# Layer-0 cross-attention prepared in eight pieces beside the units, the next stage's rows beside the last units, and a turned threshold search in a four-layer decoder

## The chip, the core and the metric

The kernel runs on one core of one Trainium2 chip. The metric is the device time of one execution in microseconds (us), and the median over several runs. The engines are named as in the profile: PE (matrix multiplications, with its weight loads as PEld), DVE (vector), ACT (scalar, activation tables), POOL (general purpose) and SP (which here issues transfers). They run side by side, each through its own queue in order, and wait for one another through semaphores. Matrix products land in PSUM, the other tiles lie in SBUF.

## The reference, cut to what matters

A decoder of four layers; each layer adds a self-attention, a cross-attention to a context and a feed-forward part to x, each behind a normalization. x is 16 sequences of 128 tokens with 256 features, the context 16 x 128 x 192, everything float32. The change touches the cross-attention and feed-forward part of layer 0, and the cross-attention and the feed-forward part of layer 2.

```
# layer 0, cross-attention (16 heads of 16); query is layernorm(x), key = value = context
Qp = query @ Wq + bq
K = _l2norm(key @ Wk + bk);  V = value @ Wv + bv;  Q = _l2norm(Qp)
scores = jnp.einsum('bhqd,bhkd->bhqk', Q, K) * SCALE
attn = jax.nn.softmax(scores, axis=-1)
out = ... einsum('bhqk,bhkd->bhqd', attn, V) ... @ Wo + bo
x = out + Qp
return (x - mu) / jnp.sqrt(var + LN_EPS) * ln_gamma + ln_beta

# layer 2, feed-forward: each of 8 experts takes the 256 tokens that score highest for it
probs = jax.nn.softmax(xt @ Wg, axis=-1)
_, top_idx = jax.lax.top_k(probs.T, cap)            # cap = 2048 // 8
tok2exp = where(assigned, argmax(masked, axis=0), argmax(pT, axis=0))
h = jax.nn.gelu(xt @ W1[e], approximate=False) @ W2[e]   # times the gate of the token
```

The feed-forward part of layer 0 has 32 routed experts of width 128 and one shared one, applied to all tokens and weighted per token.

## The kernel before

The 16 sequences are blocks of 128 tokens (a tile `self.x[g][:, t, :]` of 128 partitions by 256); four blocks are a group, so there are `NG` = 4 groups of `GB` = 4 blocks. Stages run one after the other. The framework schedules the instructions of each engine from the program's order and their dependencies; instructions recorded with `pinned` or `pinned_transpose` keep the program's order on PE, those of `mm` and `transpose_group` may be moved.

**Layer-0 attention.** `staggered` walks over the 16 blocks ("units"). For unit n it issues the scores (`scores16`, tile st16), then parts of older units, then the exponentials on ACT, then the first part of the combination of unit n-1. `combine16` is a generator with four parts: values times weights (o16, copied to oT by ACT), the turn back (o16t, `rsum` and `c` on DVE), the next turn (ctr, copied to cT by DVE), and the output projection (proj). One whole group is prepared by `prologue(g + 1)` at the third unit of group g. In the cross-attention, `prologue` computes the keys kT and the lengths of their rows (squares on ACT, `ksum` by products with a column of ones, `over_length`), the values (`values32`), the normalized rows h and their transposes hT, the queries qp with their squares on ACT, their lengths, the unit rows u on POOL (`nc.gpsimd.tensor_scalar`, line 530), and their transposes qm. After the last block of a group, `done` normalizes the group on DVE and ACT and runs three additions or products over the group on POOL (lines 548 to 550), of which the last updates x.

**Layer-0 feed-forward.** `tokens(g)` normalizes a group and turns it; `first` computes gate and up products of an expert for a group, `router` the weights, `second` the down product. `tokens(0)` and `tokens(1)` stand at the head of the stage, `tokens(2)` and `tokens(3)` behind the first two routers.

**Layer-2 cross-attention** (`xattn64`, 8 heads, 16 units) takes an optional `begin`, which returns work to be issued beside given units; here it is called without it.

**Layer-2 feed-forward** (`l2_ffn`) writes zeros to the DRAM rows `hs` (23 blocks), normalizes the groups into `hall`, turns them, and computes the logits with the tokens on the partitions (16 products of 8 columns a group, of two records each in the trace). After the softmax it seeks for each expert the largest bit pattern `thr` that at least 256 probabilities reach, two bits a step, 15 steps:

```python
nc.vector.tensor_tensor(mask, p3 (x3), cand.bitcast(F) (x16), ALU.is_ge)     # 128 x 384, bf16
self.mm(ps, [(onesb, mask)])                                                 # sum over the partitions
nc.vector.tensor_reduce(count, ps, AX.X, ALU.add)                            # sum over the 16 blocks
```

followed by three small operations on `count`, `step` and `thr` and one on `cand`. Then `ranks` numbers the chosen tokens, POOL scatters the rows of `hall` to `hs` (16 indirect transfers), and `fetch` reads blocks of `hs` in fours and the expert's weights W12 block by block.

Two pools matter: `slot` hands out one of 7 weight slots in rotation (tag w8), and `b1` one of 4 PSUM banks.

Of the kernel before, what the change touches and what calls it, by code (L numbers as in the profile page):

```python
# [16 lines left out]
P = 128  # L17
B = 16
# [11 lines left out]
class Decoder:  # L30
    def __init__(self, ctx, tc, a, out):
# [8 lines left out]
        self.flip = 0  # L40

# [218 lines left out]
    def values32(self, wk, pairs, bias):  # L260

        nc = self.nc
        v = wk.tile([P, 16, 32], F, tag="v32", name="v32", bufs=6)
        nc.gpsimd.memset(v[:, :, 16:32], 0.0)
        nc.gpsimd.memset(v[:, :, 16:17], 1.0)
        ps = self.b1("v")[:, 0:DM]
        self.mm(ps, pairs)
        nc.vector.tensor_tensor(
            v[:, :, 0:16], ps.rearrange("p (h d) -> p h d", h=16), bias.rearrange("p (h d) -> p h d", h=16), ALU.add
        )  # L270
        return v
# [107 lines left out]
    def staggered(self, prologue, maxima, scores, exponentials, combine):  # L379
# [3 lines left out]
        state = {0: prologue(0)}  # L383
# [7 lines left out]
        for n in range(B + 3):  # L391
            g, t = divmod(n, GB)
            if n < B:
                st = scores(state[g], t)
            part(n - 3)
            part(n - 2)
            if n < B:
# [6 lines left out]
            last = es  # L404
            part(n - 2)
            if t == GB - 2 and g + 1 < NG:
                state[g + 1] = prologue(g + 1)

# [75 lines left out]
    def l0_xattn(self):  # L484
# [5 lines left out]
        def over_length(n, scale):  # L490

            nc.vector.tensor_scalar(n, n, 1e-24, None, ALU.max)
            nc.scalar.activation(n, n, AF.Sqrt, scale=scale)
            nc.vector.reciprocal(n, n)

        with self.tc.tile_pool(name="l0x", bufs=1) as wk:
            bq, bv, bo = (self.brow(wk, f"L0_xattn_{n}") for n in ("bq", "bv", "bo"))

            def prologue(g):

                kT = wk.tile([P, 2, GT], F, tag="kT", name="kT", bufs=2)
                sq = self.hp.tile([P, 2, GT], F, tag="hT", name="ksq", bufs=5)
                for half in range(2):
                    ps = self.b1("kT")
                    self.mm(ps, self.ctx_l(wk_, half * P, (half + 1) * P, slice(g * GT, (g + 1) * GT)))
                    nc.vector.tensor_scalar(kT[:, half, :], ps, self.c("L0_xattn_bk")[:, half : half + 1], None, ALU.add)
                    nc.scalar.activation(sq[:, half, :], kT[:, half, :], AF.Square)
                ps = self.b1("ksum")[:, 0:GB]
                for t in range(GB):
                    self.mm(ps[:, t : t + 1], [(sq[:, half, T4(t)], self.ones[:, 0:1]) for half in range(2)])  # L510
                rk = self.small([P, GB], "rk")
                nc.vector.tensor_copy(rk, ps)
                over_length(rk, 16.0)
                v = [
                    self.values32(wk, self.ctx_r(wv, 0, DM, slice(g * GT + t * P, g * GT + (t + 1) * P)), bv)
                    for t in range(GB)
                ]
                hT = self.hidden_T(self.layernorm(g))
                qp = wk.tile([P, GB, DM], F, tag="qp", name="qp", bufs=2)
                n = self.small([P, GB], "l2n")  # L520
                junk = wk.tile([P, DM], BF, tag="junk", name="junk", bufs=1)
                for t in range(GB):
                    ps = self.b1("qp")[:, 0:DM]
                    self.mm(ps, [(hT[:, k, T4(t)], wq[:, k, :]) for k in range(2)])
                    nc.vector.tensor_tensor(qp[:, t, :], ps, bq, ALU.add)
                    nc.scalar.activation(junk, qp[:, t, :], AF.Square, accum_out=n[:, t : t + 1])
                over_length(n, 1.0)
                u = self.hp.tile([P, GB, DM], F, tag="h", name="unit", bufs=2)
                for t in range(GB):
                    nc.gpsimd.tensor_scalar(u[:, t, :], qp[:, t, :], n[:, t : t + 1], None, ALU.mult)  # L530
                qm = wk.tile([P, 2, 2, GT], F, tag="qm", name="qm", bufs=2)
                for half in range(2):
                    ps = self.b1("utr")
                    for t in range(GB):
                        nc.tensor.transpose(ps[:, T4(t)], u[:, t, half * P : (half + 1) * P], self.ident)
                    nc.vector.tensor_scalar(qm[:, half, 0, :], ps, self.par[:, 0:1], None, ALU.mult)
                    nc.scalar.activation(qm[:, half, 1, :], ps, AF.Copy, scale=self.par[:, 1:2])
                nc.gpsimd.tensor_tensor(qp, qp, bo.unsqueeze(1).to_broadcast([P, GB, DM]), ALU.add)
                return qm, kT, rk, v, qp

            def combine(s, g, t, es):
# [18 lines left out]
                combine,  # L560
            )

    def l0_ffn(self):
# [20 lines left out]
        with self.tc.tile_pool(name="l0f", bufs=1) as wk:  # L584
# [3 lines left out]
            hTs = []  # L588

            def tokens(g):  # L590
                st = self.small([P, GB, 6], "bnst")
                mv = self.small([P, GB, 2], "bnmv")
                rs = self.small([P, GB], "rstd")
                nm = self.small([P, GB], "nmean")
                for t in range(GB):
                    nc.vector.bn_stats(st[:, t, :], self.x[g][:, t, :])
                    nc.vector.bn_aggr(mv[:, t, :], st[:, t, :])
                self.rsqrt(rs, mv[:, :, 1])
                nc.vector.scalar_tensor_tensor(nm, mv[:, :, 0], -1.0, rs, ALU.mult, ALU.mult)
                h = self.hp.tile([P, GB, DM], F, tag="h", name="h", bufs=2)  # L600
                for t in range(GB):
                    nc.scalar.activation(
                        h[:, t, :], self.x[g][:, t, :], AF.Identity, scale=rs[:, t : t + 1], bias=nm[:, t : t + 1]
                    )
                hT = self.hp.tile([P, 2, GT], F, tag="hT", name="hT", bufs=5)
                for k in range(2):
                    ps = self.b1("tr")
                    for t in range(GB):
                        self.pinned_transpose(ps[:, t * P : (t + 1) * P], h[:, t, k * P : (k + 1) * P])
                    nc.scalar.copy(hT[:, k, :], ps)  # L610
                hTs.append(hT)
# [81 lines left out]
            tokens(0)  # L693
            tokens(1)
            for e in range(-1, E):
                for g in range(NG):
# [4 lines left out]
                    if e < 0:  # L701
                        router(g)
                        if g + 2 < NG:
                            tokens(g + 2)
# [975 lines left out]
    def l2_xattn(self):  # L1680
        self.xattn64(8, [f"L2_xattn_{n}" for n in ("Wq", "Wk", "Wv", "Wout")], "L2_xattn_bout", "l2x")

    def l2_ffn(self):
# [7 lines left out]
        wg = self.wp.tile([P, 2, E], F, tag="wg2", name="wg2")  # L1691
        self.load_into(wg, "L2_ffn_Wg")
        hs = self.tc.dram_tile([NB * P, DM], F, name="hs")
        ys = self.tc.dram_tile([NB * P, DM], F, name="ys")
        with self.tc.tile_pool(name="l2f", bufs=1) as wk:
            tile_ = lambda shape, name, dt=F, bufs=1: wk.tile(shape, dt, tag=name, name=name, bufs=bufs)
            zero = tile_([P, DM], "zero")
            nc.gpsimd.memset(zero, 0.0)
            for b in range(NB):
                nc.sync.dma_start(out=hs[b * P : (b + 1) * P, :], in_=zero)  # L1700
# [5 lines left out]
            bits = tile_([P, 15, 3, E], "bits", I32)  # L1706
            for i in range(15):
                for j in range(3):
                    nc.gpsimd.memset(bits[:, i, j, :], (j + 1) << (2 * i))
# [15 lines left out]
            h = tile_([P, B, DM], "hall")  # L1725
            logits = self.b1("logits")[:, 0 : B * E]
            for g in range(NG):
                hg = h[:, g * GB : (g + 1) * GB, :]
                self.norm_tokens(self.x[g], hg)
                hT = self.hidden_T(hg)  # L1730
                for t in range(GB):
                    o = (g * GB + t) * E
                    self.mm(logits[:, o : o + E], [(hT[:, k, t * P : (t + 1) * P], wg[:, k, :]) for k in range(2)])

            p3 = tile_([P, B, E], "p3")
            flat = lambda a: a.rearrange("p t e -> p (t e)")
            m = self.small([P, B], "m16")
            l3 = logits.rearrange("p (t e) -> p t e", e=E)
            nc.vector.tensor_reduce(m, l3, AX.X, ALU.max)
            bcast = lambda a: a.unsqueeze(2).to_broadcast([P, B, E])  # L1740
            over_t = lambda a: a.unsqueeze(1).to_broadcast([P, B, E])
            nc.vector.tensor_tensor(p3, l3, bcast(m), ALU.subtract)
# [7 lines left out]
            thr = tile_([P, E], "thr", I32)  # L1750
            nc.vector.memset(thr, 0)
            cand = tile_([P, 3, E], "cand", I32)
# [683 lines left out]
```

## Time and profile before

| | |
|---|---|
| median of 3 runs | 3641.01 us (3630.87 to 3645.12) |
| the profiled execution | 3646.33 us, of which the span is 3644.6 us |
| mean granted clock of TensorE | 0.948 |
| busy: PE, DVE, ACT, POOL | 3348.9, 2113.7, 1421.1, 456.9 us |
| instructions in the span | 51429 |
| layer-0 cross-attention, first kT to first gate | 181 to 380 us |
| layer-2 cross-attention to the first block of its feed-forward | 2065 to 2361 us |

The page gives the busy time of each engine, a strip of 40 equal slices, and the groups of instructions with their mean duration and what ended the idle time before them. The chain of waits follows the execution back from its last instruction. A window adds up the busy time of a stretch; its granted clock is 1.00 at full speed.

### The profile page before, as it was taken

The numbers are of one execution on the slowest core, as the hardware profiler recorded it, in microseconds if no ns is written. First come the engines' busy times: TensorE is split into PE (matmuls) and PEld (weight loads), VectorE is DVE, ScalarE is ACT, GpSimd is POOL, SyncE is SP. The second block draws the span as 40 slices with busy tenths as digits, with TensorE's granted clock in tenths as the row PEclk, the third lists the DMA queues.
The fourth block names the chain that finished last, engine by engine and source line by source line (L and its number), as shares of the span: only waits on it lengthen the run. The fifth ranks groups of instructions, "written<-read, shape, count | busy, mean of one in ns | idle before, by whom it ended". The sixth has DMA issues, their size and how long they took to land.

```text
span 3644.6 us, 51429 instructions
## 1 busy us (share of the span) xinstructions
PE 3348.9 (92%) x20976; PEld 1807.7 (50%) x20976; DVE 2113.7 (58%) x4137; ACT 1421.1 (39%) x1910; POOL 456.9 (13%) x627
## 2 busy tenths in 40 slices
PE   7888999999998899998999999196999999999999
PEld 4655555555556656665455566062122222224656
DVE  5535544444463544458777644425899999963440
ACT  3344411111124422228555322023577777783221
POOL 5423100000002221110000110104000000002100
PEclk9988999999998999999999998597799999999989
DMA  3000000000010000010000001374212020000000
GB/s 98 1 10 1 14 18 22 18 22 18 26 54 1 28 11 1 1 30 20 12 1 12 2 1 34 121 238 115 49 26 31 11 31 11 11 1 25 1 8 18
DMA packets 90484, 105.46 MB, mean 29 GB/s; under 512 B 11364, under 2 KB 72678, under 8 KB 89990
## 3 DMA queue, kind: packets, MB, share of 16 engines
q1 hardware_dynamic: 79672, 89.71, 9.3%
q0 software_dynamic: 4224, 6.43, 0.5%
q10 hardware_dynamic: 6352, 6.03, 0.5%
q8 instruction: 165, 2.70, 0.3%
q14 instruction: 71, 0.58, 0.1%
HBM read 85.53 MB, written 16.60 MB: 28 GB/s over the span
## 4 chain that ended last, share of the span: by engine, by line
PE 79%; DVE 10%; ACT 5%; issue 3%; POOL 2%; DMA 1%; SPq 0%; POOLq 0%; ACTq 0%; DVEq 0%
PE acc L1968 7%; PE down L255 6%; PE gate L255 6%; PE up L255 6%; PE proj L255 6%; PE st L1968 5%; PE one L1968 4%; PE qT L166 4%; PE st L255 4%; PE o L255 2%; PE h L255 2%; DVE mx L2114 2%; PE rb L255 2%; PE v L948 2%; PE fc L166 2%
## 5 line engine op out<-in xcount | busy, mean ns | idle before, releaser
L2114 DVE TENSOR_REDUCE mx<-one 128x1 f32<-128x512 f32 x1024 | 659.0, 686 | 62.4 <-PE one L1968 53.1
L2251 ACT ACTIVATE e<-st 128x1024 f32<-128x1024 f32 x512 | 497.0, 1021 | 214.4 <-PE st L1968 213.4
L674 ACT ACTIVATE gs<-gate,cols 128x512 f32<-128x512 f32 x132 | 90.7, 687 | 552.7 <-PE gate L255 552.6
L1968 PE MATMUL acc<-e,v 128*32 128x512 f32 x2048 | 289.6, 615 | 0.9 <-ACT e L2251 0.9
L688 DVE SCALAR_TENSOR_TENSOR x<-down,w_all,x 128x256 f32<-128x256 f32 x512 | 212.4, 478 | 111.1 <-PE down L255 110.9
L1968 PE MATMUL st<-qp,kp 113*128 113x512 bf16 x1024 | 274.5, 389 | 2.3 <-ACT e L2251 1.9
L255 PE MATMUL down<-expert,gs 128*128 128x256 f32 x1056 | 251.0, 381 | 2.2 <-DVE gs L675 2.2
L255 PE MATMUL gate<-hT,expert 128*128 128x512 f32 x528 | 250.3, 596 | 0.0
L255 PE MATMUL up<-hT,expert 128*128 128x512 f32 x528 | 248.7, 593 | 0.0
L255 PEld LDWEIGHTS down<-expert,gs 128*128 128x128 f32 x1056 | 201.4, 191 | 86.1 <-issue 61.5
L675 DVE SCALAR_TENSOR_TENSOR gs<-up,cols,gs 128x512 f32<-128x512 f32 x132 | 99.0, 750 | 230.0 <-PE up L255 229.9
L1968 PE MATMUL one<-kp,qp 16*128 16x512 bf16 x1024 | 211.9, 400 | 4.0 <-DVE mx L2114 2.6
L1968 PEld LDWEIGHTS <-qp 16*128 16x128 bf16 x1024 | 48.9, 91 | 333.4 <-issue 328.5
L255 PEld LDWEIGHTS up<-hT,expert 128*128 128x128 f32 x528 | 100.8, 191 | 127.2 <-issue 126.9
L1968 PEld LDWEIGHTS <-kp 113*128 113x128 bf16 x1024 | 79.2, 98 | 140.9 <-issue 82.6
L1048 ACT COPY rb<-rb 128x512 f32<-128x512 f32 x64 | 37.5, 586 | 258.9 <-PE rb L255 258.9
L1050 DVE TENSOR_TENSOR cT<-o,rb 128x512 f32<-128x512 f32 x64 | 44.3, 691 | 157.1 <-ACT rb L1048 157.1
L255 PEld LDWEIGHTS gate<-hT,expert 128*128 128x128 f32 x528 | 100.4, 192 | 70.5 <-issue 64.0
L166 PE MATMUL qT<-hT,L_xattn_Wq 128*128 128x512 f32 x256 | 114.1, 599 | 6.6 <-DVE hT L110 4.5
L255 PE MATMUL o<-e,v 128*32 128x128 f32 (+1 forms) x2048 | 105.6, 280 | 11.8 <-DVE nm L292 11.8
L1357 DVE SCALAR_TENSOR_TENSOR xs<-xBC,cols,xs 128x508 f32<-128x508 f32 x144 | 106.0, 741 | 12.4 <-ACT xs L1353 9.1
L962 POOL CAST kb<-kT 128x512 bf16<-128x512 f32 x64 | 41.5, 676 | 433.6 <-DVE kT L110 433.6
(522 smaller groups left out, 5512.1 us busy)
## 6 DMA issues: line engine op xcount, KB each, us to landing
W<-in_L_ffn_W_dram SPq DMA_DIRECT2D x46, 512.0 KB, 5.5
expert<-in_L_ffn_Wg_dram SPq DMA_DIRECT2D x32, 128.0 KB, 2.2
expert<-in_L_ffn_Wu_dram SPq DMA_DIRECT2D x32, 128.0 KB, 2.3
expert<-in_L_ffn_Wd_dram SPq DMA_DIRECT2D x32, 128.0 KB, 2.3
parts<-parts SPq DMA_DIRECT2D x16, 256.0 KB, 2.5
qp<-parts SPq DMA_DIRECT2D x28, 128.0 KB, 3.7
kp<-parts SPq DMA_DIRECT2D x12, 256.0 KB, 7.7
hs<-zero SPq DMA_DIRECT2D x23, 128.0 KB, 1.9
```

Source lines behind the costliest of these rows:

```text
L166: self.nc.tensor.matmul(out, lhsT, rhs, start=i == 0, stop=i == n - 1 and bias is None)
L255: self.tc.keep_in_program_order(self.nc.tensor.matmul(*a, **k))
L674: nc.scalar.activation(gs, pg, AF.Silu, bias=bg)
L675: nc.vector.scalar_tensor_tensor(gs, pu, bu, gs, ALU.add, ALU.mult)
L688: nc.vector.scalar_tensor_tensor(xt, pd[:, t, :], w_all[:, o : o + 1], xt, ALU.mult, ALU.add)
L948: nc.tensor.matmul(ps, l, r, start=True, stop=False)
L962: nc.gpsimd.tensor_copy(kb[:, i + j, :], kT[:, i + j, :])
L1050: nc.vector.tensor_tensor(cT, po, rb, ALU.mult)
L1357: stt = lambda *a: pin(nc.vector.scalar_tensor_tensor(*a))
L1968: self.tc.keep_in_program_order(nc.tensor.matmul(*a, **k))
L2114: nc.vector.tensor_reduce(mx[:, t, kc, i : i + 1], pair[i], AX.X, ALU.max)
L2251: nc.scalar.activation(e[:, 2 * p : 2 * p + 2, :], ps, AF.Exp, scale=1.0 / 16.0)
```

## The change

1. `staggered` accepts a `prologue` that is a generator. For each unit of group g two pieces of the prologue of group g + 1 are issued: one between the older units' parts and the exponentials, one behind the combination's first part; what is left is issued at the group's last unit. `beside` holds further work for given units.
2. The prologue of the layer-0 cross-attention is cut into eight pieces by `yield`. All its products are pinned. The statistics of two groups are taken together; the key lengths and query lengths share one square root; the unit rows are on DVE instead of POOL; `qp` lies in two of the weight slots.
3. `tokens` of the layer-0 feed-forward becomes the method `l0_ffn_rows`; groups 0 and 1 are issued beside units 13 and 14 of the cross-attention.
4. `l2_ffn_begin` is passed to the layer-2 cross-attention: it issues the zero writes, takes two weight slots for `hall`, and returns the statistics, rows and logits of groups 0 to 2 for the units 10, 11, 12, 14 and 15. The logits have the experts on the partitions (`lT`, 32 rows a group) and are turned back once. Group 3 is done at the head of `l2_ffn`.
5. The search runs on the turned probabilities `pT` (one partition for each pair of block and expert, 128 tokens along the row); the count over the row comes from the compare's accumulator, the sum over the 16 blocks from one product with `same`.
6. The count of `above` is one product instead of `ranks`; `fetch` reads the first block of `hs` alone and then fours.

```diff
 # staggered
+            ahead = not whole and g + 1 < NG
+            if ahead and t == 0:
+                pieces = prologue(g + 1)
             if n < B:
                 st = scores(state[g], t)
             part(n - 3)
             part(n - 2)
+            if ahead:
+                piece(g + 1)
             if n < B:
                 es = exponentials(state[g], t, st, nm)
...
             last = es
+            if ahead:
+                piece(g + 1)
             part(n - 2)
-            if t == GB - 2 and g + 1 < NG:
+            if whole and t == GB - 2 and g + 1 < NG:
                 state[g + 1] = prologue(g + 1)
+            while ahead and t == GB - 1 and g + 1 not in state:
+                piece(g + 1)
+            for work in (beside or {}).get(n, ()):
+                work()
 # l0_xattn, prologue
+                if g in (0, 2):
+                    stats([g, g + 1])
+                mv, rs = rows[g]
...
-                    self.mm(ps, self.ctx_l(wk_, half * P, (half + 1) * P, slice(g * GT, (g + 1) * GT)))
+                    products(ps, self.ctx_l(wk_, half * P, (half + 1) * P, slice(g * GT, (g + 1) * GT)))
...
                     nc.scalar.activation(sq[:, half, :], kT[:, half, :], AF.Square)
+                    yield
...
+                nc.vector.tensor_scalar(n[:, 0], ps, 1e-24, 16.0, ALU.max, ALU.mult)
+                yield
+                if g % 2 == 0:
+                    qps.append(self.slot([P, 2, GB, DM], "qp"))
...
-                over_length(n, 1.0)
+                nc.vector.tensor_scalar(n[:, 1], n[:, 1], 1e-24, None, ALU.max)
+                nc.scalar.activation(n, n, AF.Sqrt)
+                nc.vector.reciprocal(n, n)
                 u = self.hp.tile([P, GB, DM], F, tag="h", name="unit", bufs=2)
                 for t in range(GB):
-                    nc.gpsimd.tensor_scalar(u[:, t, :], qp[:, t, :], n[:, t : t + 1], None, ALU.mult)
+                    nc.vector.tensor_scalar(u[:, t, :], qp[:, t, :], n[:, 1, t : t + 1], None, ALU.mult)
...
+                yield
...
+                {13: [lambda: self.l0_ffn_rows(0)], 14: [lambda: self.l0_ffn_rows(1)]},
 # l2_ffn_begin
+        h = [self.slot([P, 8, DM], "hall") for _ in range(2)]
...
+            r = slice(32 * g, 32 * g + 32)
+            ps = self.b1("lT")
+            for k in range(2):
+                self.pinned(ps[r, :], wg[:, k, :], hT[:, k, :], start=k == 0, stop=k == 1)
...
+        st["last"] = [lambda: stats([3]), lambda: rows(3), lambda: logits(3)]
+        return {
+            10: [at(stats, [0, 1]), at(rows, 0)],
+            11: [at(rows, 1), at(logits, 0)],
+            12: [at(logits, 1)],
+            14: [at(stats, [2]), at(rows, 2)],
+            15: [at(logits, 2)],
+        }
 # l2_ffn
+            ps = self.b1("pT")[:, 0:P]
+            self.pinned_transpose(ps, flat(p3))
...
             for i in range(14, -1, -1):
+                nc.vector.tensor_tensor(cand, bits[:, i], thr.bitcast(I32).to_broadcast([P, 3]), ALU.bitwise_or)
+                for j in range(3):
+                    nc.vector.tensor_scalar(
+                        mask, pT, cand.bitcast(F)[:, j : j + 1], 0.0, ALU.is_ge, ALU.add, accum_out=count[:, j : j + 1]
+                    )
+                ps = self.b1("count")[:, 0:3]
+                self.pinned(ps, flat(same), count, start=True, stop=True)
+                nc.vector.scalar_tensor_tensor(best[:, 0:3], ps, CAP - 0.5, cand.bitcast(F), ALU.is_ge, ALU.mult)
+                nc.vector.tensor_reduce(thr, best, AX.X, ALU.max)
```

## The prediction

> **What bounds the kernel now.** I read the page first, then the windows of 5 us through the layer-0 cross-attention, then the chain of waits through that stage and through the gate of the last mixture-of-experts stage, and last the timelines of the same stretches.
>
> ```profile
> PE 3348.9 (92%) x20976; PEld 1807.7 (50%) x20976; DVE 2113.7 (58%) x4137; ACT 1421.1 (39%) x1910; POOL 456.9 (13%) x627
> ...
> PE   7888999999998899998999999196999999999999
> ...
> PEclk9988999999998999999999998597799999999989
> ```
>
> TensorE carries the kernel nearly everywhere. A slice is 91 us. Two places stand out: slices 3 and 4 (182 to 364 us, layer-0 cross-attention), where PE is at 8 and the clock at 8, and slice 26 (2278 to 2369 us, the layer-2 gate), where PE is at 1 and DVE at 9. The change works on these two alone, so the sum is made stage by stage.
>
> Windows of 5 us; after the two times come the length, busy PE, PEld, DVE, ACT, POOL, the granted clock, and DMA:
>
> ```profile
> 265.00:270.00 5.00, 4.97 (x16) 1.97 (x15) 3.97 (x9) 1.96 (x5) 3.19 (x2) 1.00 0.00 0
> 270.00:275.00 5.00, 5.00 (x21) 3.04 (x20) 5.00 (x7) 0.09 (x1) 3.85 (x2) 0.66 0.00 0
> 275.00:280.00 5.00, 5.00 (x15) 2.83 (x14) 2.18 (x6) 0.28 (x2) 0.00 (x0) 0.50 0.00 0
> 280.00:285.00 5.00, 4.47 (x16) 3.39 (x16) 1.70 (x4) 1.96 (x7) 0.00 (x0) 0.82 0.00 0
> 285.00:290.00 5.00, 1.60 (x7) 0.73 (x7) 0.35 (x2) 0.71 (x3) 3.63 (x5) 0.87 0.00 0
> 290.00:295.00 5.00, 5.00 (x25) 3.40 (x26) 1.70 (x3) 3.71 (x5) 2.34 (x1) 0.50 0.02 3
> ```
>
> This is one prologue of a group. PE loses twice: it idles 3.4 of 5 us at 285 (waiting for POOL's unit rows), and it runs at half clock from 271.6 to 281.8 and from 288.6 to 295.5 (windows of 0.5 us place the edges, which lie multiples of 3.4 us apart). The chain, start and length in us:
>
> ```profile
> 264.15 4.02 PE kT L166 x8
> ...
> 271.40 6.50 PE v L166 x12
> ...
> 279.80 4.68 PE qp L166 x16
> ...
> 286.29 3.63 POOL unit L530 x4
> ...
> 290.65 2.02 PE st L255 x16
> ...
> 309.06 4.02 PE kT L166 x8
> ...
> 356.33 2.38 POOL qp L548
> ...
> 361.24 2.37 POOL x L550
> 363.62 0.43 DVE bnst L596
> ...
> 379.74 3.41 PE gate L255 x4
> ```
>
> A period (kT to kT) is 44.9 us; the end of the stage is a serial chain to the first `gate`. In the layer-2 gate:
>
> ```profile
> 2251.69 3.26 DVE hall L205 x6
> ...
> 2279.99 0.57 DVE mask L1760
> 2280.60 0.49 PE count L166
> ...
> 2282.56 0.57 DVE mask L1760
> ```
>
> The search begins 28.6 us after the last residual add (2251.35), and one of its 15 steps takes 2.59 us (2279.99 to 2282.56), 38.9 in all.
>
> **The change part by part.** Durations are of the profiled execution (3646.3 us, span 3644.6); the median of the three runs, 3641.0, is 5.3 below it.
>
> *Group periods.* Nothing is removed from PE: at full clock a prologue is kT 4.0, transposes 0.9, ksum 0.3 + 1.7, qp 3.4 (its adds follow at 0.86 a token), v 5.0 (1.2 to 1.3 a token at 268), unit transposes 0.9: 16.2 us. Four units are 4 x (st 1.07, proj 1.06, o16t 0.44, o 1.05, ctr 0.40) = 16.1. So 32.3 us at full clock and without waits, against 44.9. The idle wait at 285 goes, since units run beside the qp, length and unit steps; what is late next is DVE. The unit rows move from POOL (3.63 us for four) to DVE, four at 0.35 by the `qp` rows of L205 (1.38 for four). They and the `h` rows then stand in DVE's one queue ahead of `cT`, for which PE's `proj` waits. The price of that is in this row (DVE, layer-0 stages):
>
> ```profile
> L205 DVE TENSOR_SCALAR h<-x,bnmv,rstd 128x256 f32<-128x256 f32 x12 | 13.2, 1150 | 0.1
> ```
>
> 1150 ns instead of 350: at 269 to 274 these rows stood while POOL ran its 2.35 us adds. PE has st, v and o as cover (about 5 us), so I charge 1.5 us a period; bounds 0 and 5.
>
> *Clock, where a rule and the trace part.* In the trace the clock fell at 271.6 with PE never idle: what preceded was ksum, 14 records one column wide, 1.7 of the 3.4 us before the edge. The Trainium skill, "TensorE: Matmul & The Clock Gate", Part 1, says that an idle window of about 3.4 us throttles; by that rule, filling the hole removes all half-clock time, and a period is 33.8. By the row, ksum trips it again, now among eight transposes and `o16`: one or two windows of 3.4 us at half clock, which cost half of that, say 3.0 (bounds 0 and 6). I follow the row: 32.3 + 1.5 + 3.0 = 36.8, a gain of 8.1 in each of two periods. The first (209.45 to 245.40, 36.0) has few older units to finish: about 11 + 16.2 + 3 = 30; gain 6.
>
> *First prologue* (181.65 to 209.45, 27.8): nothing to run beside. kT 4.0, transposes and the second square 1.5, ksum 2.0, qp 5.4, two v 3.5 over the length, unit and transpose steps, 0.9, two v 3.5: 20.8. Gain 7, between 4 and 9.
>
> *End of the stage.* From unit 12 to the last proj (335.56 to 367.55) rows 0 and 1 of the next stage add 16 transposes (1.8), on ACT eight `h` and four copies, and between the last two exponentials a pair of table loads (1.28 each): some 6 us later for unit 15. But this runs while DVE would have stood at `bnst` for POOL's group-2 chain (356.3 to 363.6) anyway; net loss 1. Then the first `gate` follows at once, and the next thing late is group 3's transpose: add, statistics, norm 2.9, POOL 7.1, statistics 2.4, square root and `h` 3, queueing 3: 18.5 after the last proj, against 27.4 now (367.55 to 394.94). Gain 8.9. The stage in all: 7 + 6 + 16 - 1 + 9 = 37, bounds 18 and 50.
>
> *Gate of layer 2.* Three of four groups' transposes and logits go beside the attention units: 8 transposes (0.9) and two products 512 wide (4 records at 0.43) are 2.6 us each, 7.9 on a PE that is full there (49.4 of 50 us); one table-load pair less there gives back 1.3 (the hole at 2237). For group 3: add, statistics 1.1, a wait for POOL's `bits` memsets (they end 2.5 us after the pool opens) 1.6, norm 1.6, transposes and copies 1.9, half-clock product 3.4, copy and turn back 1.6, softmax 2.0, turned probabilities 0.9: 13.7 instead of 28.6. Net 14.9 - 6.6 = 8.3; bounds 4 and 11.
>
> *Search step.* It loses the 0.56 mask and the 0.56 reduction, gains three compares of 128 wide with a sum. No row has a DVE sum. Neighbouring compares 128 wide start 0.21 apart (2318.6). By rows alone: candidates 0.22, compares 0.66, PE and hops 0.6 (mask end to reduction start is 0.57 now), scale 0.22, maximum 0.22: 1.92. The skill's "VectorE: DVE Perf Modes", section "Two Vector instructions with no wait between them", counts an operation that writes its accumulator as two instructions; MATCH_VALUE_LOAD, a second half of that kind, takes 0.08 here, and ACT's accumulator read 0.19. That speaks against the change: 1.92 + 3 x 0.08 = 2.16. I take 2.16: 15 x 0.43 = 6.5, between 3 (with 0.16 each) and 10. After the search a transpose adds 0.6 and a shorter count removes about 0.2; the first block's load, 128 instead of 512 KB, saves 1.4 of 3.7. Together 16, bounds 8 and 24.
>
> *Costed at nothing.* The 23 zero writes (0.54 us of SP each, 12.4) now stand before the Wv and Wout loads of the attention; those were issued at 1984 and are wanted near 2078, so 90 us cover them; uncovered they cost 12. Two weight slots hold `qp`, and the experts' loads now stand behind the bias rows in SP's order (182 instead of 25 us), four experts ahead instead of five: they are wanted at 368, land in 2.3, and an expert takes 4 x 5.2. Two slots hold `hall`: blocks 5 and 6 wait for the scatters (2356) and are wanted near 2383. If a cover went, some 3 us each.
>
> **Sum.** 37 + 16 = 53: 3646.3 becomes 3593, and with the 5.3 to the median 3588.
>
> **The rivals.** (a) *New waits take half.* DVE held by POOL's adds, ACT's table loads between exponentials, four PSUM buffers in rotation: periods of 41.5, nothing at the end; 15 + 12 = 27, so 3614. For it: the 1150 ns row, and the fixed PE order. Against: DVE would be busy some 23 of 37 us a period, ACT 20. Chance 0.13. (b) *Slower: the clock stays low through the stage.* If thin pieces (transposes, ksum, 32-wide `o16`) sit in every window, PE never wins its clock back: periods 32.3 x 2 = 65, so 3 x 20 lost and the 9 of the end gone, 16 won: +44, 3685. It decides from a half-clock share of about two thirds of the stage (33.8 + 32.3 c = 55 sets the loss against the other gains). For it: v in the prologue ran 10 us at half clock without recovering. Against: from 100 to 150 us the layer-0 self-attention mixes units and transposes with clock 1.00. Chance 0.05. (c) *The stages overlap already, so little moves* (the unpinned products were mixed with v before): within 18 us, 0.02. The forecast has 0.80.
>
> **Numbers.** Bounds of the parts give 26 to 74 off the profile, so 3567 to 3615; with the runs' spread (3631 to 3645) and rival (a), 3560 to 3616. A measurement of this kernel tells about 0.5%, 18 us: faster 0.88, the same 0.07 (part of (a), and (c)), slower 0.05.
>
> **What would show it.** Right: POOL's `unit` gone, no PE hole of over 3 us before `st` of a group's first unit, st to st over four units near 37, clock over 0.9 between 210 and 330; `gate` directly behind the last proj; search steps of 2.1 to 2.2. Wrong: clock at 0.5 across whole periods, PE waiting for `cT` or `e` in each unit, steps over 2.5, or the layer-2 attention longer by more than 10.

## The result and the profile after

The changed kernel takes 3602.9 us (median of 4 runs, 3594.8 to 3607.8) against 3640.3 (4 runs, 3630.9 to 3645.1): ratio 0.9898, 95% interval 0.9871 to 0.9925, so 27 to 47 us faster. The prediction said 3588, within 3560 to 3616, faster. The sign held, and of the 53 us it summed, 37 came; by its parts the result is nearer to its rival (a) than to the forecast, as "Why the prediction came out as it did" works out. The profiled execution took 3604.5 us (span 3602.7, clock 0.962), 41.8 less than the one before.

The page of the kernel after, engines and slices:

```profile
PE 3305.2 (92%) x20947; PEld 1789.6 (50%) x20947; DVE 2117.7 (59%) x4185; ACT 1415.6 (39%) x1904; POOL 443.5 (12%) x613
...
PE   7888999999998899998899999297999999999999
...
PEclk9988999999999999999999999597999999999989
```

PE's busy time fell by 43.7 us with only 29 records fewer (20947 against 20976): a record at half clock takes about twice as long (four `proj` 2.05 us at 268.05, 1.13 at 352.42), and the granted clock rose from 0.948 to 0.962. In slices 3 and 4 both rows still read 8.

The 5-us windows of one group period after (times, length, busy PE, PEld, DVE, ACT, POOL, then the clock and DMA); the `ksum` of this period runs from 248.4 to 250.2:

```profile
245.00:250.00 5.00, 5.00 (x49) 4.50 (x48) 2.70 (x7) 3.34 (x4) 0.00 (x0) 1.00 0.00 0
...
255.00:260.00 5.00, 5.00 (x52) 3.55 (x51) 3.88 (x14) 4.56 (x10) 0.53 (x3) 1.00 0.01 2
260.00:265.00 5.00, 2.62 (x22) 1.36 (x22) 4.28 (x6) 3.60 (x4) 4.84 (x3) 1.00 0.00 0
265.00:270.00 5.00, 1.95 (x5) 1.52 (x6) 5.00 (x4) 0.00 (x0) 4.44 (x2) 0.74 0.01 3
270.00:275.00 5.00, 5.00 (x48) 3.96 (x46) 4.34 (x13) 1.18 (x3) 0.47 (x3) 0.58 0.00 0
```

The old hole ahead of the unit transposes and `st` is gone. A new one stands at 262.6: PE idles 5.4 us, until 268.05, while DVE and POOL are both "busy", and the clock is at half from 267.4 to 274.2. The timeline (start, length) says why:

```profile
259.96 2.36 POOL L619 TENSOR_TENSOR qp<-qp,bcast 128x1024 f32<-128x1024 f32 x1 [0.66 <-DVE lengths L583]
261.55 6.02 DVE L588 TENSOR_SCALAR unit<-qp,lengths 128x256 f32<-128x256 f32 x4
262.40 2.35 POOL L620 TENSOR_TENSOR qp<-qp,bcast 128x1024 f32<-128x1024 f32 x1
264.82 2.34 POOL L621 TENSOR_TENSOR x<-x,qp 128x1024 f32<-128x1024 f32 x1
267.49 0.41 DVE L373 COPY cT<-ctr 128x256 f32<-128x256 f32 x1
```

Four `unit` rows take 6.02 us, one slipping in between each two of POOL's operations (0.91, 2.50, 2.49 and 0.34 one by one); one period earlier, with POOL quiet, the same four took 1.14 (223.51). POOL keeps its 2.35 us. `cT` stands behind the rows in DVE's queue, and PE's `proj` waits for `cT`. So a "busy" DVE is here a DVE that waits.

The end of the stage, in the chain of waits (start, length):

```profile
352.42 1.15 PE proj L257 x4
...
356.80 2.36 POOL qp L619
359.22 2.35 POOL qp L620
361.65 2.35 POOL x L621
364.02 0.43 DVE bnst L643
...
365.20 0.61 ACT h L649
...
368.66 2.34 PE gate L257 x4
```

The shared expert's first `gate` does run right behind the last proj (353.4; the `gate` above is a later one), but then PE idles 7.2 us (358.7 to 365.9): DVE waits at `bnst` of group 3 for POOL's `x`, and the reciprocal that group 2's rows need stands behind it in the queue.

One search step after, in the timeline:

```profile
2255.77 0.35 DVE L1902 TENSOR_SCALAR_CACHE_REDUCE mask<-pT,cand 128x128 bf16<-128x128 f32 x1
2256.04 0.08 DVE L1902 DVE_READ_ACCUMULATOR mask<-pT,cand 128x1 f32 x1
2256.16 0.35 DVE L1902 TENSOR_SCALAR_CACHE_REDUCE mask<-pT,cand 128x128 bf16<-128x128 f32 x1
...
2257.58 0.16 DVE L1907 SCALAR_TENSOR_TENSOR best<-count,cand 128x3 f32<-128x3 f32 x1 [0.68 <-PE count L257]
2257.78 0.16 DVE L1908 TENSOR_REDUCE best<-best 128x1 f32<-128x4 f32 x1
2257.97 0.16 DVE L1900 TENSOR_TENSOR cand<-bits,best 128x3 int32<-128x3 int32 x1
2258.17 0.34 DVE L1902 TENSOR_SCALAR_CACHE_REDUCE mask<-pT,cand 128x128 bf16<-128x128 f32 x1
```

Compares start 0.39 apart, and a step takes 2.41 (14 steps from 2253.30 to 2287.0), not 2.16.

**Where the 41.9 us of span lie**, by like events in the two traces: layer-0 cross-attention from the first `kT` to the last `router` product 18.8, and 0.1 ahead of it; from there to layer 2's cross-attention 2.0; to its first expert block 12.5; the blocks 0.9; layer 3 7.6, where nothing was changed. These 7.6 need explaining too.

For the layer-0 stage all kernels are cut at the same seven marks: first `kT`, `st` of units 0, 4, 8 and 12, start of the last proj, last router product. (The marks 245.40, 290.65 and 335.56 of the prediction are units 3, 7 and 11, since the old prologue stood ahead of those; it calls 335.56 unit 12. Only the split between its terms shifts by this, not their sum.)

| kernel | kT to 0 | 0 to 4 | 4 to 8 | 8 to 12 | 12 to proj | to router | sum |
|---|---|---|---|---|---|---|---|
| before | 28.1 | 42.5 | 44.9 | 44.7 | 24.7 | 43.1 | 228.0 |
| after | 20.6 | 32.2 | 43.0 | 40.4 | 34.8 | 38.2 | 209.2 |
| after, once more | 20.6 | 32.2 | 43.0 | 40.4 | 34.8 | 38.2 | 209.1 |
| layer-0 part alone | 22.3 | 28.7 | 38.9 | 40.4 | 34.1 | 39.5 | 203.8 |
| layer-2 part alone | 23.7 | 40.4 | 46.9 | 44.9 | 24.7 | 41.5 | 222.0 |
| unit rows on ACT | 21.2 | 27.0 | 40.1 | 35.3 | 37.0 | 39.6 | 200.2 |
| unit rows with a sum | 22.2 | 42.6 | 40.6 | 35.1 | 36.9 | 38.4 | 215.7 |
| adds on DVE, one batch | 19.5 | 27.9 | 38.4 | 37.6 | 37.3 | 35.3 | 196.0 |
| no rows beside | 22.3 | 28.7 | 38.9 | 39.8 | 24.7 | 39.5 | 193.8 |
| rows two units later | 20.6 | 32.4 | 42.5 | 38.9 | 31.9 | 38.5 | 204.9 |
| adds on DVE, spread | 19.5 | 27.9 | 33.4 | 33.4 | 32.4 | 35.0 | 181.7 |
| spread, no rows beside | 19.5 | 27.9 | 33.4 | 33.4 | 27.1 | 45.2 | 186.5 |

### The profile page after: what moved, and what is told of

It is laid out like the page before. It is cut to its first block, busy times and chain, and to the rows that moved or that the text cites. A ratio compares the mean times of both kernels' runs of the same rounds, so it can differ in the third digit from the quotient of the medians.

```text
span 3602.7 us, 51438 instructions
## 1 busy us (share of the span) xinstructions
PE 3305.2 (92%) x20947; PEld 1789.6 (50%) x20947; DVE 2117.7 (59%) x4185; ACT 1415.6 (39%) x1904; POOL 443.5 (12%) x613
## 4 chain that ended last, share of the span: by engine, by line
PE 78%; DVE 9%; ACT 5%; issue 4%; DMA 2%; POOL 1%; SPq 0%; POOLq 0%; ACTq 0%; DVEq 0%
PE acc L2110 7%; PE down L257 6%; PE gate L257 6%; PE up L257 6%; PE proj L257 6%; PE st L2110 5%; PE one L2110 4%; PE st L257 4%; PE qT L168 4%; PE o L257 3%; PE h L257 2%; DVE mx L2256 2%; PE rb L257 2%; PE fc L168 2%; PE pr L168 2%
## 5 line engine op out<-in xcount | busy, mean ns | idle before, releaser
L1120 ACT COPY rb<-rb 128x512 f32<-128x512 f32 x64 | 37.5, 585 | 256.6 <-PE rb L257 256.6
L257 PE MATMUL o<-e,v 128*32 128x128 f32 (+1 forms) x2048 | 105.4, 279 | 13.7 <-DVE nm L294 11.8
L257 PEld LDWEIGHTS o<-e,v 128*32 128x32 f32 (+1 forms) x2048 | 81.5, 124 | 29.7 <-POOL e L335 12.3
```

Of the source, the lines that this page charges most:

```text
L257: self.tc.keep_in_program_order(self.nc.tensor.matmul(*a, **k))
L1120: nc.scalar.copy(rb, ps)
```

## The experiments

Ratios are to the kernel before on the same chip, with 95% intervals.

**The two parts alone.** No line is edited; each kernel takes one half of the diff.

> The kernel before with the layer-0 part of the change alone (prologue in eight pieces, rows beside the last units). Landmark tables of the two profiles give this part 20.4 us (first centers product of layer 1), against the 37 of the prediction. Theory: 3641 - 20 = 3621, and the 9 us that the changed kernel's profile gains at the start of the layer-3 attention, where nothing was changed, is the clock coming back earlier by chance: any value from -2 to 9 here. Rival: those 9 us belong to the layer-2 part; then none here, and 9 more in the kernel with that part alone.

> The kernel before with the layer-2 part alone (logits beside the attention, turned search, block list earlier). Landmarks give this part 13.5 us up to the first block of the experts (5.9 up to the search, 2.3 in the search, 4.3 behind it, 0.9 in the blocks): 3641 - 13.5 = 3627; with the layer-3 clock as a part of it (rival) 3618. Together with the layer-0 part alone the gains should add to the 37 of the changed kernel within the spread of 5.

Layer-0 part: 0.9944 (0.9925 to 0.9964), 20 us. Layer-2 part: 0.9972 (0.9958 to 0.9986), 10 us. Together 30, within the interval of the 37. Up to the first block the layer-2 part gives 11.8 us here (296.4 from `kT` to the first block, now 284.5), 12.5 in the changed kernel. Layer 3 took 1140.1 and 1140.7 us in these profiles, as before (1140.5): its 7.6 us belong to neither part.

**The changed kernel once more.**

> The changed kernel once more, unaltered. The clock's half-speed stretches are whole multiples of 3.41 us, and where they begin differs from profile to profile. Theory (phase): its layer-0 stage, 209.2 us from the first kT to the last router in the first profile and 203.8 in the kernel with the layer-0 part alone, comes out anywhere from 200 to 212, and the start of the layer-3 attention has either 48 or 72 us of half clock; the median stays 0.990 of before. Rival (the differences belong to the code): 209 and 48 again within 1 us.

0.9900 (0.9880 to 0.9920): the ratio repeats. Windows at the start of the layer-3 attention, first profile and then second (the same instructions lie 2 us apart in them):

```profile
2542.00:2547.00 5.00, 5.00 (x21) 0.89 (x20) 5.00 (x10) 2.08 (x3) 0.00 (x0) 1.00 1.03 115
```

```profile
2539.00:2544.00 5.00, 5.00 (x15) 0.82 (x16) 3.53 (x7) 1.84 (x2) 0.50 (x1) 0.50 1.06 121
2544.00:2549.00 5.00, 5.00 (x14) 0.53 (x10) 3.52 (x6) 1.23 (x2) 0.00 (x0) 0.50 0.80 95
2549.00:2554.00 5.00, 5.00 (x15) 0.76 (x14) 2.74 (x5) 1.02 (x1) 0.00 (x0) 0.50 0.00 0
2554.00:2559.00 5.00, 5.00 (x14) 0.82 (x12) 3.68 (x6) 1.26 (x2) 0.00 (x0) 0.50 0.00 0
```

One kernel, 47.8 us of half clock in this stretch in the one profile and 71.7 in the other; layer 3 takes 1132.9 and 1140.4. So the 7.6 us were not the change's. In the layer-0 stage the same spread was expected; it did not show here (209.1), but the layer-0 part alone, with the same code there, has 203.8. In all, the changed kernel has 10.2 us more at half clock there (47.8 against 37.5), worth half of that; the stretch that the other lacks begins at 229.8:

```profile
225.00:230.00 5.00, 3.18 (x48) 2.35 (x46) 5.00 (x9) 1.54 (x3) 2.59 (x3) 0.98 0.00 0
230.00:235.00 5.00, 5.00 (x17) 2.52 (x20) 1.78 (x5) 1.54 (x3) 0.04 (x1) 0.50 0.01 3
```

and the same stretch of the kernel with the layer-0 part alone:

```profile
225.00:230.00 5.00, 3.19 (x43) 2.09 (x42) 4.76 (x11) 1.55 (x4) 1.70 (x3) 1.00 0.00 0
230.00:235.00 5.00, 5.00 (x33) 2.90 (x33) 2.41 (x8) 2.73 (x4) 0.00 (x0) 1.00 0.02 3
```

Both have the same hole of 1.8 us (at 226.6 and 225.6). What sets the difference is open: the two profiles of the changed kernel agree to 0.1 us. Stages are therefore compared below by their waits, and with the 203.8 where a profile lacks this stretch.

**The unit rows off the shared port.** Two ways: on ACT, and on DVE in a form that writes a sum.

```diff
-nc.vector.tensor_scalar(u[:, t, :], qp[:, t, :], n[:, 1, t : t + 1], None, ALU.mult)
+nc.scalar.activation(u[:, t, :], qp[:, t, :], AF.Copy, scale=n[:, 1, t : t + 1])          # first
+nc.vector.tensor_scalar(u[:, t, :], qp[:, t, :], n[:, 1, t : t + 1], 0.0, ALU.mult,
+                        ALU.add, accum_out=us[:, t : t + 1])                             # second
```

> Changed kernel with its four unit rows a group on ScalarE (activation Copy with a scale) instead of VectorE; nothing else. Theory A (VectorE's rows wait for GpSimd's adds): the row that took 5.9 us at 261.6 and 301.9 goes, the hole of TensorE ahead of proj (5.4 us at 262.6) shrinks to under 2, and with it the half-clock window behind it (some 2.5 us); the h rows (3.4 us) stay and now stand nearer to the adds, so 5 of the 8 us come back in each of two groups: 8 to 12 us faster than the changed kernel, 3591 to 3595. Theory B (the hole comes from TensorE's fixed order and the clock, whoever writes the rows): within 3 us of 3603.

> Changed kernel with the four unit rows still on VectorE and in the same place of its queue, but as the form that also writes a sum (one more tile of four columns, not used). By the Trainium skill, 'SBUF - State Buffer', the form with an accumulator does not enter the mode that takes the port shared with GpSimd. If the port is what holds the rows: each 0.43 us (0.35 and 0.08), four 1.7 instead of 5.9, and nearly the time of the kernel with the rows on ScalarE, 3592 to 3597. If GpSimd's adds slow any VectorE operation on rows in SBUF: 5.9 us as before and 3603 or more.

On ACT: 0.9892 (0.9870 to 0.9913), not to be told from the changed kernel's 0.9898 and 0.9900; its 3594.9 us lies in the range named, but the kernel before was 5 us faster on that chip too. With the sum: 0.9922 (0.9904 to 0.9941), 3606.4 us, a miss. Neither brought 8 us. The timelines, first ACT, then the sum:

```profile
251.53 1.71 ACT L588 ACTIVATE unit<-qp,lengths 128x256 f32<-128x256 f32 x4 [0.32 <-DVE lengths L585]
252.93 7.75 DVE L546 TENSOR_SCALAR h<-x,l1mv,l1rs 128x256 f32<-128x256 f32 x4
```

```profile
270.48 2.36 POOL L622 TENSOR_TENSOR qp<-qp,bcast 128x1024 f32<-128x1024 f32 x1 [0.65 <-DVE lengths L583]
...
272.07 0.47 DVE L589 TENSOR_SCALAR_CACHE_REDUCE unit<-qp,lengths 128x256 f32<-128x256 f32 x1
272.47 0.08 DVE L589 DVE_READ_ACCUMULATOR unit<-qp,lengths 128x1 f32 x1
...
272.92 2.36 POOL L623 TENSOR_TENSOR qp<-qp,bcast 128x1024 f32<-128x1024 f32 x1
274.00 6.51 DVE L546 TENSOR_SCALAR h<-x,l1mv,l1rs 128x256 f32<-128x256 f32 x4
```

These rows show the mechanism: with a sum, four rows take 1.6 us while POOL runs (rows 0.40 apart), in the same place of the same queue; without it 6.0. So the form of the row decides, and not POOL's traffic as such. The Trainium skill, "SBUF — State Buffer", section "Who interferes with whom", says that the form that writes its sum does not take the port that DVE shares with POOL, and the trace agrees. But the next rows in DVE's queue, `h` of the group after, now meet the adds and take 7.75 and 6.51 instead of 3.4. The hole of that period only moved, from `proj` to `o` (5.1 and 4.3 us). In the last period, which has no further group and so no `h` rows, it does go: 35.3 and 35.1 from unit 8 to 12 instead of 40.4. The second kernel's profile also holds 27 us of half clock from 198.5, against 3.4 from 202.5 in the changed kernel. They begin just behind the unit rows of its first prologue (196.2 to 197.9); whether the longer rows there set them off was not tried, so its total says little about the port.

**POOL's adds on DVE, in one batch.**

```diff
-nc.gpsimd.tensor_tensor(qp, qp, gamma..., ALU.mult)      # and beta, and x; 128x1024 each
+for i in range(GB): nc.vector.tensor_tensor(qp[:, i, :], qp[:, i, :], gamma, ALU.mult)   # and beta, and x
-nc.gpsimd.tensor_tensor(qp, qp, bo..., ALU.add)
+for t in range(GB): nc.vector.tensor_tensor(qp[:, t, :], qp[:, t, :], bo, ALU.add)
```

> Changed kernel with the four GpSimd adds and products of a group (x gamma, + beta, into x, and + bo onto qp) done on VectorE in pieces of 256 columns, 16 pieces of about 0.35 us a group. With the rows moved to ScalarE the wait only went over to the h rows; so theory A' is that any VectorE row behind GpSimd's 9.4 us of adds waits, and that taking away the adds takes away all of it, though VectorE gets 5.6 us more a group: the 5.4 us holes and 2.5 to 3 of half clock in each of two periods, 1.8 in the first, and 3 to 5 behind the last proj, less 1 a group: 14 to 20 us, 3583 to 3589. Rival B' (VectorE becomes the bound: cT stands behind 16 more pieces): periods stay at 40 or grow, 3600 to 3610.

0.9889 (0.9868 to 0.9910), 9 us below the median of the changed kernel on the same chip (3602.4): less than expected, and the intervals overlap. In the profiles the stage is 196.0 against 203.8. Instead of one hole of 5.4 there are two of 2.5 and 1.4, the first because `cT` now stands behind twelve adds. Behind the last proj 4 us are won (35.3 against 39.5), but 3 are lost ahead of it (37.3 against 34.1), where the rows beside now leave a hole of 7.5 instead of 5.7.

**Without the rows beside the last units.**

```diff
-{13: [lambda: self.l0_ffn_rows(0)], 14: [lambda: self.l0_ffn_rows(1)]},    # in l0_xattn
+self.l0_ffn_rows(0); self.l0_ffn_rows(1)                                    # ahead of the experts' loop
```

> Changed kernel with the rows of groups 0 and 1 made at the head of the mixture-of-experts stage again, not beside units 13 and 14. By the trace of the changed kernel the rows beside cost a hole of 5.6 us and a half-clock window at unit 15 (st 12 to the last proj 34.7 us instead of 32.0), and save the head. Theory: last proj 5 to 8 us earlier, first gate 8 to 10 us later behind it; in all 0 to 5 slower, 3603 to 3608. Rival (the rows beside buy nothing because group 3's adds end the stage either way): 3 to 6 faster.

0.9868 (0.9847 to 0.9889): 3589.2 beside 3602.4 of the changed kernel on the same chip. The theory failed; the rival was right, and its 3 to 6 us too small. Unit 12 to the last proj takes 24.7 instead of 34.1, as in the kernel before, and behind the last proj it is 39.5 either way. What the rows cost beside the units is in the timeline of the changed kernel:

```profile
329.95 1.28 ACT L193 ACT_TABLE_LOAD   x1
333.25 2.34 POOL L619 TENSOR_TENSOR qp<-qp,bcast 128x1024 f32<-128x1024 f32 x1 [22.98 <-DVE rstd L194]
333.29 2.32 DVE L646 SCALAR_TENSOR_TENSOR nmean<-bnmv,rstd 128x4 f32<-128x4 f32 x1
335.70 2.08 ACT L649 ACTIVATE h<-x,nmean,rstd 128x256 f32<-128x256 f32 x4 [3.49 <-DVE nmean L646]
336.35 2.80 PE L260 MATMUL tr<-ident,h 128*128 128x128 f32 x8 [5.68 <-ACT h L649]
```

`nmean`, an operation on four columns, takes 2.32 us beside POOL's add and ends with it; with POOL quiet it takes 0.15 (364.95). ACT's `h` waits for it, PE's pinned transposes for `h`, and the scores of unit 15 stand behind those.

**The rows two units later.**

```diff
-{13: [lambda: self.l0_ffn_rows(0)], 14: [lambda: self.l0_ffn_rows(1)]},
+{15: [lambda: self.l0_ffn_rows(0)], 16: [lambda: self.l0_ffn_rows(1)]},
```

> Changed kernel with the rows of groups 0 and 1 two units later, behind units 15 and 16 instead of 13 and 14 (two numbers in the table). Without the rows beside the units the stage was 10 us shorter from the first kT to the last router (193.8 against 203.8), all of it ahead of the last proj (24.7 instead of 34.1 from st 12), and nothing was lost behind it. Theory: what cost it is the table change for the square root between two exponentials and the wait of nmean behind GpSimd's adds, in front of unit 15's scores. Behind unit 15 no exponential follows, and the stage head (4.1 us of idle TensorE before tr) is saved too: st 12 to the last proj 25 to 29, 192 to 196 in all, 10 to 14 faster than the changed kernel, 3588 to 3592. Rival (the copies and transposes themselves are the price, wherever they stand): 34 again, 3600.

0.9912 (0.9884 to 0.9940), 3596.2 us where 3588 to 3592 was expected: nothing gained in the median. The profile has the same half-clock stretch at 229 as the changed kernel's 209.2 and comes to 204.9; unit 12 to the last proj takes 31.9. The square root between exponentials and the wait in front of unit 15's scores, which this edit takes away, are thus the smaller part of the price. Behind unit 15 the rows still cost 7 of the 10 us: 3.4 of them go to a half-clock stretch (6.8 us from 334.8), and `nmean` again stands behind POOL's add, so that PE waits 2.6 and 2.0 us.

**A search step without the sum.** An added loop of 15 steps in front of the real one.

```diff
+nc.vector.tensor_scalar(bare[:, j], pT, cand.bitcast(F)[:, j : j + 1], None, ALU.is_ge)     # no accum_out
+self.pinned(ps, flat(same), bare[:, :, 0], start=True, stop=True)
```

> Changed kernel with a second search loop of 15 steps put ahead of its own, on tiles of its own, whose three compares write no sum (the product counts a single column instead, so this added loop finds nothing of use; the real search is unchanged). It measures a step without the accumulator. Theory (the accumulator is the miss): compares start 0.21 to 0.22 apart as between rows of before, a step takes 2.43 - 3 x 0.17 = 1.9 us. Rival (the hops between VectorE and TensorE are the miss): compares shorter but the step 2.2 or more. The kernel is longer by the loop, 28 to 33 us.

The step is 1.95 us, three compares together 0.68:

```profile
2253.97 0.68 DVE L1905 TENSOR_SCALAR bare<-pT,cand 128x128 f32<-128x128 f32 x3
2254.70 0.50 PEld L257 LDWEIGHTS count<-bare,same 128*128 128x128 f32 x2 [1.44 <-DVE bare L1905]
```

In the same profile a step of the real loop takes 2.40. So writing the sums costs 0.46 of the 2.41 a step, 0.15 a compare, nearly the dearer end (0.16) that the prediction named. The added loop also writes its masks in f32 instead of bf16; what that does to the time was not tried. The kernel's one run took 3630.9, with the added loop in it.

**The adds spread over units**: rows two units later, and one token's three adds (and its `bo`) with each unit of the next group.

```diff
+nc.vector.tensor_tensor(qp[:, t, :], qp[:, t, :], bo, ALU.add)
 nc.vector.tensor_tensor(qp[:, t, :], qp[:, t, :], ps, ALU.add)
+if pend: pend.pop(0)()                                   # one token of the group in front: gamma, beta, into x
 if t == GB - 1:
     self.norm_tokens(qp, qp)
-    nc.gpsimd.tensor_tensor(...)                         # three of 128x1024
+    pend.extend((lambda g=g, qp=qp, i=i: into_x(g, qp, i)) for i in range(GB))
+    while pend and g == NG - 1: pend.pop(0)()
```

> The kernel of the later rows, with GpSimd's adds on VectorE and spread: one token's three operations of 256 columns (and its bo) with each unit of the next group, the last group's at once. The adds in one batch on VectorE left holes of 2.5 and 1.4 us ahead of proj and utr, since cT stood behind twelve of them. Theory (it is a matter of what stands ahead of cT in VectorE's queue): holes under 1, periods 34 to 36, tail behind the last proj 35 instead of 39.5; first kT to last router 180 to 186 instead of 204 to 209, so 3575 to 3583. Rival (VectorE, TensorE or the clock is full anyway): periods stay at 38, 3588 to 3592.

0.9857 (0.9836 to 0.9879), 3579.7. Periods are 33.4, holes in them at most 0.9, and the clock is full through both:

```profile
255.00:260.00 5.00, 4.10 (x51) 3.19 (x50) 5.00 (x15) 1.95 (x4) 0.44 (x2) 1.00 0.02 3
260.00:265.00 5.00, 5.00 (x34) 2.96 (x32) 4.54 (x15) 2.97 (x5) 0.00 (x0) 1.00 0.00 0
265.00:270.00 5.00, 5.00 (x46) 2.00 (x44) 2.54 (x8) 1.33 (x3) 0.44 (x2) 1.00 0.00 0
```

DVE does more work than in the changed kernel and is full in the first of them, and it costs little: PE waits 0.6 us for `cT` and 0.9 for `qp`.

**Spread, and the rows at the head again.** The edit is that of the kernel without the rows beside.

> The kernel with the adds spread on VectorE, and the rows of groups 0 and 1 at the head of the mixture-of-experts stage instead of beside the last units. With the adds on GpSimd the rows beside cost 9.4 us ahead of the last proj and gained nothing behind it. Theory (the two act on different places, so they add): st 12 to the last proj 25 instead of 32.4, behind it 35 to 38, first kT to last router 174 to 178 instead of 181.7; 3570 to 3577 beside 3580. Rival (without GpSimd's adds the group-3 chain is short, so the head shows again behind the last proj, as the prediction had it): 42 behind it, 182 in all, no gain.

0.9848 (0.9820 to 0.9875), 3579.7: no difference to the one before that can be told. Here the rival was right: unit 12 to the last proj is 27.1, but behind it 45.2, with one hole of 9.1 us; the last group's twelve adds, ahead of `nmean` of group 0 in DVE's queue, are 4.1 of it. In the profiles the rows beside the units thus win 4.8 us of the stage once the adds are off POOL (181.7, with them behind units 15 and 16, against 186.5), and cost 10 while they are on it; the medians show the second, not the first.

By their medians both spread kernels beat the two given ones. Against the changed kernel, measured on other chips, their ratios are lower by 0.004 to 0.005, some 15 to 19 us, with intervals that overlap the first of the changed kernel's (from 0.9871) a little and the second (from 0.9880) no more.

## Why the prediction came out as it did

- *First prologue*: 20.8 predicted, 20.6 measured. Right.
- *Holes of the periods*: the first failed term. It charged 1.5 us for DVE rows ahead of `cT`, because PE would have 5 us of cover, and gave 0 and 5 as bounds. Measured: PE idle 5.4 us in two of the three periods. The working had the 1150 ns row, and priced a row, not the queue: POOL's chain of three is 7 us long, and one row fits between two of its operations, so four rows last nearly as long as the chain. Rival (a) named this mechanism.
- *Clock*: 3.0 us a period was the right size by luck (a stretch of 6.8 us in each of two periods, half of it lost). In the changed kernel the clock is full through each ksum beside units (211, 248 and 289) and falls within the 5.4 us holes, 4.8 us into the first and 2.1 into the second. With the holes filled a period is 33.4: that is the 33.8 that the Trainium skill's rule gave ("TensorE: Matmul & The Clock Gate", Part 1), not the 36.8 of the row followed in the forecast. Not all is in the rule: in the first prologue the clock still falls right behind ksum (188.9), with 0.4 us idle ahead of it.
- *Periods in all*: 30, 36.8 and 36.8 predicted. By the marks of the table one unit of the end (4.0 us, a quarter of the prediction's 16.1) belongs to the first period, so the forecast is 34, 36.8 and 36.8; measured 32.2, 43.0 and 40.4. That is 8 of the 19 us by which the terms of this stage fell short.
- *End of the stage*: by the same marks, unit 12 to the end of the last proj 29 predicted, 35.9 measured; from there to group 3's transposes 18.5 predicted, 22.6 measured: the other 11. The failed step is "this runs while DVE would have stood at `bnst` anyway; net loss 1". Without the rows beside, those units are 9.4 us shorter. That the rows bring nothing behind the last proj in turn (39.5 with and without) is because PE then waits 7.2 us for group 2's rows, where without them it waits 4.1 for group 0's. Predicted "the next thing late is group 3's transpose": it was group 2's, held by the order of DVE's queue.
- *Gate of layer 2*: 8.3 predicted, 5.9 measured. The head is 13.5 (2239.79 to 2253.30), predicted 13.7 (its terms add to 14.1); the attention grew from 186.3 to 195.6, 9.3 instead of 6.6. The traces show where: each group's rows add 3.1 us to the units instead of 2.6, with a wait of 0.35 to 0.42 for the copy `hT` ahead of the products, and the 1.3 that one table load less was to give back did not come (PE waits 0.37 us at that place before and after).
- *Search*: 2.16 a step predicted, 2.41 measured: 2.7 us in all instead of 6.5. The failed term was the sum at 0.08 a compare; it is 0.15. The rule that such an operation is two held, and the second one's record is 0.08 long, as priced (from MATCH_VALUE_LOAD, which is the first of its pair in the trace, not the second). But the next compare starts only behind it, 0.39 after the one in front; without sums compares overlap and start 0.20 apart.
- *Behind the search*: 1.0 predicted, 4.0 measured: 0.7 less up to the first scatter, 1.6 in the last scatter's landing (4.8 to 3.2) and 1.6 in the first block's load (3.7 to 2.1). The scatter was not foreseen.
- *Costed at nothing* (zero writes, slots): PE has no hole at the attention's weights or at the blocks (98.0 us for 23, before 98.8); right.

Layer 0 came to 19 to 24 instead of 37, layer 2 to 12 instead of 16: in the profile 18 and 3.5 us short. That the total came nearer than its parts is luck: 7.6 us of layer 3's clock and 2.0 between the stages, which no term foresaw, made up for half of it.

Rival (a), given a chance of 0.13, fits better than the forecast. It named periods of 41.5 (the last two were 43.0 and 40.4), nothing won at the end (5 us were lost: unit 12 to the last router is 73.0 us, before 67.8) and 12 for layer 2 (12.5); its 3614 is 11 us above the result, the forecast 15 below. The reason held against it, that DVE would be busy only 23 of 37 us a period, counted work and not the time for which a row waits.

## What to carry to other kernels

Price a row that is moved to another engine by what runs beside it on a shared port, for the length of that whole chain, and by everything that waits behind it in its queue. Moving one victim away hands the wait to the next; ending it took moving the long operations and spreading them, so that no batch stands ahead of what PE waits for. Filling PE's time at a stage's end buys nothing where another chain sets that end.

## What the hardware showed that was not expected

- Half-clock stretches are multiples of 3.41 us, and how long they last is not fixed by the code: at the start of layer 3 the changed kernel had 47.8 us of half clock in one profile and 71.7 in another, and layer 3 took 7.5 us more. The same 1.8 us hole ahead of unit 4 was followed by 10.2 us of half clock in three profiles (after, once more, rows later) and by none in three others (layer-0 part alone, search without the sum, no rows beside), with the same code up to there; between the stages of after and of the layer-0 part alone that made 5.4 us. A single profile's difference of under 10 us is thus no evidence until the windows' clock is compared.
- At half clock PE can look fully busy (5.00 of 5) for 20 us without getting its clock back.
- An operation of four columns by 128 partitions takes 2.32 us beside POOL's add, and 0.15 without.
